# Twenty-six ranges instead of twenty-seven in a planned graph layer: a fourth of the sums per quadrant, fused counting matmuls, and one store set later in the plan

## The chip, the cores and the metric

The kernel runs on one core of one Trainium2 chip. Its time is the device time of that core in microseconds (us), given as the median of many executions; a profile holds one execution, whose span runs from its first to its last instruction. The engines are PE (TensorE, matmuls; PEld is its weight load), DVE (VectorE), ACT (ScalarE), POOL (GpSimd) and SP (SyncE, which here only issues transfers). They run side by side, each through its own list of instructions in order, and wait for one another by semaphores.

## The reference, cut to what matters

A graph has 6250 nodes with 128 features each and 100,000 edges, sorted by their destination. Each edge has one of two types.

```python
Xs = X[src]
m_data = Xs @ W_data.T + b_data
m_ctrl = Xs @ W_control.T + b_control
msg = jnp.where((edge_types == 0)[:, None], m_data, m_ctrl)
agg = jax.ops.segment_sum(msg, dst, num_segments=X.shape[0])
out = relu(agg + (X @ W_self.T + b_self))
x = layernorm(x + out)        # over the 128 features, eps 1e-5
```

A node has 16 incoming edges on average. A message depends only on the source node and the type, so there are 2 x 6250 different messages.

## The kernel before, in words

**The message table.** Up to some 60 us into the run the kernel computes all messages: 49 blocks of 128 nodes, two types, so 98 tiles of 128 rows (`NT`). Each message is kept as three bfloat16 parts of 128 columns side by side, 384 columns (`D3`), whose sum has nearly full precision. The table stays in SBUF as `m3` and is also stored to DRAM as `table`, in 13 pieces (L509). The last piece is the single odd block.

**Two ways to sum.** The nodes are cut in two. The first 27 x 160 = 4320 nodes form 27 ranges ("windows" in the code, `NW` of `WN` = 160 nodes). The other 1930 nodes are cut in 16 blocks of 125 nodes (`GN`), the last one of 55.

*A range* is summed from `m3` by selection matmuls. First the edges of a group of ranges (`GROUPS`: one, then two, then six groups of four) are *ranked* (`ranks`): 21 chunks of 128 edges are turned into one-hot rows over the 98 tiles, and chains of matmuls on `tri` and `rest` (L702) with a maximum on DVE between them (L716) give each edge a slot, at most 32 for each tile. Groups 0 and 1 split the 21 chunks in 4 and 2 chains, and matmuls on `every`, a matrix of ones, add the counts of the earlier chains first. All these matmuls go out as quartets: four matmuls, each with 32 columns of weights, one per quarter (quadrant) of the array's columns. A scatter of 21 matmuls for each range (L752) writes the packed slots to PSUM, ACT copies them to `vs` (L765), and SP stores them to DRAM as `packed` (`put`, L772, L774). SP then loads them back for each range, spread over all partitions (`rows`, L904, 784 KB), and DVE turns them into selection matrices (L912); a second set, `hot2`, comes from L920.

Then `sums` goes over the 25 groups of four tiles (g = 0 to 24, the last with two). Stage 1 (L933) picks the rows with a quartet of 384-column matmuls into a PSUM tile `g`; ACT, at times DVE, copies this to `gs` (L436); stage 2 adds it to the accumulator `a` of the range. The first 128 nodes take a quartet of 384 columns (L947). The remaining 32 nodes take three matmuls of 128 columns (L950), one for each of the three parts; they go to three quadrants, in the columns of the bank behind the first 384. At the end of the range these 96 x 128 values are copied to `bs`, and in `close` a float32 matmul on `fold`, three 32 x 32 identities on top of each other, adds the three parts for the 32 nodes (L552). `close` also adds the own term, the residual and the normalization, and stores the result. The 32 leftover nodes of all ranges of a group are closed together, as a block; the range of group 0 is closed with those of group 1, so there are seven blocks.

*A block of 125 nodes* is summed by gathering (`gathered`): for each 128 edges POOL issues an indirect load of 128 table rows (L1027), into one of 14 `t_msg` buffers, and a quartet on PE adds them to the block's sums by a one-hot matrix (L1034). With some room for the spread of the counts a full block takes 17 such gathers and the last one 8, so 263 in all. Besides these, 14 smaller gathers fetch `sr`, the few edges whose slot did not fit (L861).

**Who sets the order.** `Plan` writes the order of all engines out before the program is built. Every piece of work (`add`) has an engine, a duration, a due time, what it reads and writes. The planner simulates the engines and always lets the engine take the ready piece with the earliest due time; the instructions are then issued in the order of the planned starts. So the durations and due times are no time of the chip, but they set the order. The planned duration of a gather is `GC`; gathers get due times `step` apart, and `step` is the larger of `GC` + 0.02 and the time of the ranges shared out over all gathers. Transfers on SP take 0.45 us in the plan (`SPD`). Some SP transfers with a due time over 60 also have a `slack`: they are ready that much later than their inputs, so that they don't stand at the head of SP's queue waiting. The stores of `packed` are among these, with 2.0; that of group 1 has a due time of 25.7 and so no slack.

## Time and profile before

| | us |
|---|---|
| median of 14 runs | 696.29 (693.05 to 698.5) |
| the profiled execution | 693.26 |
| its span | 691.7 |
| PE busy (matmuls) | 530.7, 77% |
| DVE busy | 398.4, 58% |
| ACT busy | 359.3, 52% |
| POOL busy | 287.6, 42% |
| mean granted clock of TensorE | 0.909 |

Busy time is the time in which at least one instruction of the engine ran. Matmuls overlap, so PE's share says how long PE had work, not how much it got done; for that one counts matmuls in a stretch. A wait is put down to the engine whose semaphore came last. In a row such as `a<-gs,hot 128*32 128x384 bf16 x4` the weights are 128 x 32 and the moving operand is 128 x 384, and x4 is the number of instructions merged in the row. The granted clock is 1.00 or 0.50 in a stretch.

### The profile page before, as it was taken

The numbers are of one execution on the slowest core, as the hardware profiler recorded it, in microseconds if no ns is written. First come the engines' busy times: TensorE is split into PE (matmuls) and PEld (weight loads), VectorE is DVE, ScalarE is ACT, GpSimd is POOL, SyncE is SP. The second block draws the span as 40 slices with busy tenths as digits, with TensorE's granted clock in tenths as the row PEclk, the third lists the DMA queues.
The fourth block names the chain that finished last, engine by engine and source line by source line (L and its number), as shares of the span: only waits on it lengthen the run. The fifth ranks groups of instructions, "written<-read, shape, count | busy, mean of one in ns | idle before, by whom it ended". The sixth has DMA issues, their size and how long they took to land.

```text
span 691.7 us, 26926 instructions
## 1 busy us (share of the span) xinstructions
PE 530.7 (77%) x11461; PEld 374.4 (54%) x11461; DVE 398.4 (58%) x1271; ACT 359.3 (52%) x891; POOL 287.6 (42%) x290
## 2 busy tenths in 40 slices
PE   6999458838778587876878876888778798686893
PEld 4666225626566274654556654666446475464672
DVE  6899336827678185767256674676546374532432
ACT  3657215615456273545545564655446364464783
POOL 1100454264453636355363436445543545553510
PEclk9999677977999699999798999999989999798997
DMA  3797622253423333315234142551414412532311
GB/s 105 225 334 240 196 62 67 51 172 108 134 59 116 87 111 104 116 46 157 78 105 118 50 140 72 144 137 48 154 52 116 124 48 66 179 94 63 109 32 26
DMA packets 63117, 76.83 MB, mean 111 GB/s; under 512 B 21000, under 2 KB 52893, under 8 KB 62989
## 3 DMA queue, kind: packets, MB, share of 16 engines
q1 hardware_dynamic: 49147, 47.35, 22.4%
q0 software_dynamic: 13456, 27.42, 14.6%
q8 instruction: 91, 1.49, 0.9%
q10 hardware_dynamic: 386, 0.26, 0.2%
q14 instruction: 37, 0.30, 0.2%
HBM read 60.50 MB, written 13.17 MB: 107 GB/s over the span
## 4 chain that ended last, share of the span: by engine, by line
PE 68%; ACT 10%; issue 9%; another core or an unknown queue 7%; DVE 3%; DMA 1%; ACTq 0%; DVEq 0%
PE g L933 19%; PE a L947 19%; PE ga L1034 8%; ACT gs L436 8%; PE rk L702 8%; PE a L950 4%; PE vt L752 2%; PE g L493 2%; ACT to_d L443 1%; PE a L493 1%; PE a L518 1%; DVE slot L716 1%; PE ga L702 1%; DMA rows<-packed 1%
## 5 line engine op out<-in xcount | busy, mean ns | idle before, releaser
L436 ACT CAST gs<-g 128x384 bf16<-128x384 f32 x639 | 278.9, 481 | 256.3 <-PE g L933 112.0
L1027 POOL DMA_INDIRECT t_msg<-table,t_idx x263 | 269.1, 1023 | 313.8 <-PE ga L1034 161.5
L947 PE MATMUL a<-gs,hot 128*32 128x384 bf16 x2592 | 263.4, 349 | 98.5 <-ACT gs L436 58.2
L933 PE MATMUL g<-m,rows 128*32 128x384 bf16 x2646 | 277.9, 348 | 15.2 <-issue 13.1
L947 PEld LDWEIGHTS <-hot 128*32 128x32 bf16 x2700 | 124.2, 98 | 169.8 <-issue 150.0
L933 PEld LDWEIGHTS <-rows 128*32 128x32 bf16 x2646 | 164.6, 136 | 37.8 <-issue 24.0
L950 PE MATMUL a<-gs,hot 128*32 128x128 bf16 x1944 | 167.0, 228 | 4.4 <-issue 4.3
L716 DVE TENSOR_REDUCE slot<-rk 128x4 f32<-128x392 f32 (+1 forms) x138 | 77.0, 558 | 113.8 <-PE g L933 39.0
L1034 PE MATMUL ga<-t_msg,t_hot 128*32 128x384 bf16 x1036 | 109.9, 341 | 5.5 <-issue 5.5
L950 PEld LDWEIGHTS <-hot 128*32 128x32 bf16 x2025 | 83.8, 100 | 14.4 <-issue 8.4
L920 DVE TENSOR_TENSOR hot<-iota_b,to_d 128x1280 bf16<-128x1280 bf16 (+1 forms) x81 | 67.3, 841 | 0.0
L702 PE MATMUL rk<-hots,tri 128*32 128x392 bf16 (+1 forms) x588 | 62.1, 327 | 1.4 <-issue 1.4
L702 PE MATMUL rk<-hots,rest 128*32 128x392 bf16 (+1 forms) x556 | 57.5, 331 | 6.2 <-DVE slot L716 3.9
L1021 DVE TENSOR_TENSOR t_hot<-iota_b,t_code 128x768 bf16<-128x768 bf16 (+2 forms) x47 | 24.8, 528 | 58.8 <-PE g L933 31.2
L1034 PEld LDWEIGHTS <-t_hot 128*32 128x32 bf16 x1036 | 48.4, 100 | 18.8 <-issue 14.5
L561 DVE TENSOR_REDUCE s<-a 128x128 f32<-128x384 f32 x27 | 15.0, 557 | 55.4 <-ACT bs L436 37.2
L691 DVE TENSOR_TENSOR hots<-iota_b,st 128x784 bf16<-128x784 bf16 (+1 forms) x83 | 39.1, 488 | 13.0 <-PE rk L702 8.0
L702 PEld LDWEIGHTS <-rest 128*32 128x32 bf16 x624 | 25.6, 98 | 20.4 <-issue 17.8
L912 DVE TENSOR_SCALAR rows<-rows,pid 128x1568 bf16<-128x1568 bf16 x54 | 34.0, 635 | 2.8 <-DMA rows<-packed 2.8
L702 PEld LDWEIGHTS <-tri 128*32 128x32 bf16 x672 | 27.8, 98 | 7.3 <-issue 5.0
L861 POOL DMA_INDIRECT sr<-table,at x14 | 14.4, 1030 | 39.9 <-DVE at L849 26.6
L752 PE MATMUL vt<-hots,two 128*64 128x98 bf16 x546 | 18.8, 209 | 3.3 <-issue 2.8
(188 smaller groups left out, 527.7 us busy)
## 6 DMA issues: line engine op xcount, KB each, us to landing
rows<-packed SPq DMA_DIRECT2D x27, 784.0 KB
table<-m SPq DMA_DIRECT2D x12, 768.0 KB
t_msg<-table,t_idx POOLq DMA_INDIRECT x263
rows<-in_xt SPq DMA_DIRECT2D x8, 256.0 KB
xc<-in_xt SPq DMA_DIRECT2D x6, 320.0 KB
gl<-sr SPq DMA_DIRECT2D x27, 48.0 KB
xr<-in_x SPq DMA_DIRECT2D x5, 256.0 KB
out<-xr SPq DMA_DIRECT2D x5, 256.0 KB
```

The source lines that it names most:

```text
L436: [("ACT", act(cols), lambda: A.copy(o(), src())), ("DVE", dve(cols), lambda: V.tensor_copy(o(), src()))], None, None, due, r, w, lat)
L691: lambda k=k, kn=kn, ci=ci, hs4=hs4: V.tensor_tensor(hv(ci)[:, k - ks[ci] : k - ks[ci] + kn].rearrange("p k w (c d) -> p (k w) c d", d=2), ...
L702: T.matmul(acc.t[R * j : R * j + R, c * wide : c * wide + wide], wt.t[:, R * j : R * j + R], one(k).rearrange("p w c -> p (w c)"), start=s ...
L716: vec(due, len(m) * wide, lambda r=r, m=m: V.tensor_reduce(slot.t[:, r:KT:L, :], acc.t[:, : len(m) * wide].rearrange("p (k w c) -> p k w c ...
L752: T.matmul(vv()[q : q + 64, i // 2, :], two.t[:, (k - k0) * nw + i].rearrange("p f r -> p (f r)"), one(k)[:, i, :], start=k == 0 and i < 2 ...
L912: add("DVE", dve(half * NT, 0.335), lambda sp=sp, rs=rs: V.tensor_scalar(sp.t[:, rs], sp.t[:, rs], pid1.t, None, op0=ALU.is_equal), due - ...
L920: lambda i=i, hot2=hot2, s4=s4, c0=c0, c1=c1: V.tensor_tensor(hot2.t[:, c0:c1].rearrange("p g (c d) -> p g c d", d=2), iota1_b.t.rearrange ...
L933: T.matmul(gp.t[R * t : R * t + R, :D3], sp.t[:, :, 4 * g + t], m3.t[:, 4 * g + t, :], start=True, stop=True)
L947: T.matmul(a.t[R * j : R * j + R, :D3], hot2.t[:, g, R * j : R * j + R], gs.t, start=g == 0, stop=False, skip_group_check=True)
L950: T.matmul(a.t[R * c : R * c + R, D3:], hot2.t[:, g, P:], gs.t[:, c * D : (c + 1) * D], start=False, stop=last, skip_group_check=True)
L1027: add("POOL", GC, lambda m=m, kk=kk: G.indirect_dma_start(out=m.t, out_offset=None, in_=table[:, :], in_offset=bass.IndirectOffsetOnAxis(a ...
L1034: T.matmul(ga.t[R * i : R * i + R, :D3], hot.t[:, k % KB, R * i : R * i + R], m.t, start=k == 0, stop=False, skip_group_check=True)
```

## The change

Seven edits in one:

1. **26 ranges.** `GROUPS` ends in five groups of four and one of three. 26 x 160 = 4160 nodes remain with the ranges; the other 2090 make 17 blocks, sixteen with 17 gathers and one of 90 nodes with 13, so 285 gathers.
2. **Fourths instead of thirds.** The 384 columns of `gs` for the last 32 nodes of a range are cut in four pieces of 96 (`Q`), one for each quadrant, instead of three of 128. The accumulator's tail is 128 x 96.
3. **The fold follows.** `fold` and its two DVE instructions go. In `close`, float32 matmuls on 32-column slices of the identity add the pieces: cut at every multiple of 96 and of 128, there are six segments (96, 32, 64, 64, 32, 96 columns) for each range, where there was one of 128.
4. **Fused counts.** In `ranks` the matmuls on `every` for the chains behind a chunk are one matmul with a repeated operand instead of one for each chain. For group 0 that is 18 quartets of up to 294 columns instead of 36 of 98. Group 1, with two chains, has as many as before.
5. **The planner's gather duration** is 1.26 instead of 1.3, so `step` goes from 1.32 to 1.28.
6. **The planner's durations** for the changed matmuls: stage 2 0.206 instead of 0.22, the block's fold 1.0 instead of 0.6.
7. **The store of group 1's packed slots** gets a slack of 3.0 in the plan.

```diff
-GROUPS = [1, 2] + [4] * 6
+GROUPS = [1, 2] + [4] * 5 + [3]
...
+    Q = D3 // 4
...
-    GC = 1.3
+    GC = 1.26
...
-    fold = C([3 * R, R], F32, "fold")
-    vec(30, R, lambda: V.tensor_add(fold.t, ident.t[: 3 * R, 0:R], ident.t[: 3 * R, R : 2 * R]),
-        [ident], [fold])
-    vec(30, R, lambda: V.tensor_add(fold.t, fold.t, ident.t[: 3 * R, 2 * R : 3 * R]),
-        [ident, fold], [fold])
...
-                for j, (_, bs) in enumerate(block):
-                    T.matmul(o(j, R), fold.t, bs.t, start=True, stop=False, skip_group_check=True)
+                first_ = True
+                for at in sorted({*range(0, D3, Q), *range(0, D3, D)}):
+                    q, f0 = at // Q, at % D
+                    n = min(Q - at % Q, D - f0)
+                    for j, (_, bs) in enumerate(block):
+                        T.matmul(f.t[R * j : R * j + R, f0 : f0 + n],
+                                 ident.t[:, R * q : R * q + R],
+                                 bs.t[:, at % Q : at % Q + n], start=first_, stop=False,
+                                 skip_group_check=True)
+                    first_ = False
...
-            add("PE", 0.6, mms, due, [xb, w_sb, one3, brows, fold] + [b for _, b in block], [f])
+            add("PE", 1.0, mms, due, [xb, w_sb, one3, brows, ident] + [b for _, b in block], [f])
...
-        def add_to(c, wt, k, start, stop):
+        def add_to(c, wt, k, start, stop, n=1):
             for j in range(4):
-                T.matmul(acc.t[R * j : R * j + R, c * wide : c * wide + wide],
-                         wt.t[:, R * j : R * j + R], one(k).rearrange("p w c -> p (w c)"),
-                         start=start, stop=stop, skip_group_check=True)
+                T.matmul(acc.t[R * j : R * j + R, c * wide : (c + n) * wide].rearrange(
+                    "p (n c) -> p n c", n=n), wt.t[:, R * j : R * j + R],
+                    one(k).rearrange("p w c -> p (w c)")[:, None, :].to_broadcast([P, n, wide]),
+                    start=start, stop=stop, skip_group_check=True)
...
-            add("PE", (nc_ - 1 - k // L) * wide / 2400, lambda k=k: [
-                add_to(c, every, k, k == 0 and c == 1, False) for c in range(k // L + 1, nc_)], when + 1.5,
-                [hkey(k), every], [acc])
+            more = nc_ - 1 - k // L
+            add("PE", max(more * wide / 2400, 0.08), lambda k=k, more=more: add_to(
+                nc_ - more, every, k, k == 0, False, more), when + 1.5, [hkey(k), every], [acc])
...
-        add("SP", SPD, put, d2 + 1, [vs], [(packed_b, gi)], lat=2.0)
+        op = add("SP", SPD, put, d2 + 1, [vs], [(packed_b, gi)], lat=2.0)
+        if gi == 1:
+            op.slack = 3.0
...
-                    for c in range(3):
-                        T.matmul(a.t[R * c : R * c + R, D3:], hot2.t[:, g, P:],
-                                 gs.t[:, c * D : (c + 1) * D], start=False, stop=last,
+                    for c in range(4):
+                        T.matmul(a.t[R * c : R * c + R, D3 : D3 + Q], hot2.t[:, g, P:],
+                                 gs.t[:, c * Q : c * Q + Q], start=False, stop=last,
                                  skip_group_check=True)
-                add("PE", 0.22, stage2, d + 0.9, [gs, (hot2, (g >= 9) + (g >= 17))], [a])
+                add("PE", 0.206, stage2, d + 0.9, [gs, (hot2, (g >= 9) + (g >= 17))], [a])
...
-            bs = B(work, [3 * R, D], F32, "bs", 5)
-            evict(lambda bs=bs: bs.t, lambda a=a: a.t[: 3 * R, D3:], D, due + TW + 0.8, [a], [bs])
+            bs = B(work, [P, Q], F32, "bs", 5)
+            evict(lambda bs=bs: bs.t, lambda a=a: a.t[:, D3 : D3 + Q], Q, due + TW + 0.8, [a], [bs])
```

## The prediction

> **What bounds the kernel now.** I read the chain that ended last first, then the costliest groups, then how many matmuls PE got through in stretches of different granted clock, and last two short timelines. The chain and the groups, from the page:
>
> ```profile
> PE 68%; ACT 10%; issue 9%; another core or an unknown queue 7%; DVE 3%; DMA 1%; ACTq 0%; DVEq 0%
> ...
> L436 ACT CAST gs<-g 128x384 bf16<-128x384 f32 x639 | 278.9, 481 | 256.3 <-PE g L933 112.0
> L1027 POOL DMA_INDIRECT t_msg<-table,t_idx x263 | 269.1, 1023 | 313.8 <-PE ga L1034 161.5
> L947 PE MATMUL a<-gs,hot 128*32 128x384 bf16 x2592 | 263.4, 349 | 98.5 <-ACT gs L436 58.2
> L933 PE MATMUL g<-m,rows 128*32 128x384 bf16 x2646 | 277.9, 348 | 15.2 <-issue 13.1
> ```
>
> PE holds 68% of the chain. ACT's copies and POOL's gathers are idle nearly as long as they are busy, and what ends their idle time is PE. So from the end of the table (some 57 us) to 680 us PE's stream of instructions sets the time. How fast PE goes is in the table by stretch (columns: PE busy with its matmuls, PEld, DVE, ACT, POOL, the clock, DMA share, GB/s):
>
> ```profile
> 57.00:680.00 623.00, 479.75 (x10762) 341.72 (x10759) 347.18 (x1051) 327.31 (x827) 283.51 (x277) 0.91 0.36 102
> ...
> 70.00:74.30 4.30, 1.19 (x29) 0.66 (x23) 2.46 (x4) 0.96 (x2) 3.38 (x4) 1.00 1.05 347
> 74.30:88.00 13.70, 7.52 (x97) 4.72 (x100) 4.53 (x10) 3.18 (x8) 4.55 (x5) 0.50 0.45 118
> 98.20:111.90 13.70, 7.28 (x85) 4.22 (x87) 3.67 (x9) 4.61 (x10) 7.14 (x8) 0.50 0.23 59
> ...
> 660.00:680.00 20.00, 19.62 (x520) 16.04 (x511) 6.14 (x25) 17.21 (x44) 0.27 (x1) 1.00 0.10 28
> ```
>
> At the end, with little to wait for, PE does 26 matmuls in a us; over the whole stretch 17.3. The ratio, 1.5, is what waits add to PE's own pace. Part of it are stretches at half clock, in which only 6 to 7 matmuls in a us get done; the first one follows a lull of PE at 70 to 74 us.
>
> The pace itself, from PE's timeline near the end and in the first ranking:
>
> ```profile
> 676.48 0.35 PE L947 MATMUL a<-gs,hot 128*32 128x384 bf16 x4
> 676.64 0.24 PE L950 MATMUL a<-gs,hot 128*32 128x128 bf16 x3
> 676.66 0.38 PE L933 MATMUL g<-m,rows 128*32 128x384 bf16 x4
> 676.86 0.35 PE L947 MATMUL a<-gs,hot 128*32 128x384 bf16 x4
> ```
>
> ```profile
> 11.28 1.79 PE L702 MATMUL ga<-xr,every 128*32 128x98 bf16 x80
> ```
>
> One g takes 0.38 us from L947 to L947. L947 to L950 is 0.16, a quartet of 384 columns; stage 1 is as wide, so the three matmuls of 128 columns take what is left, 0.06. The 80 matmuls on `every` are 20 quartets of only 98 columns; without the last one's own 0.28 us they start within 1.51, 0.079 a quartet. By their columns that would be 0.041 (0.16 x 98/384): short quartets in a row don't go below 0.08.
>
> **The change part by part**, in PE's own time first.
>
> *The range that goes:* 25 g at 0.38, 9.5; its own term, a float32 quartet of 128 columns (two passes; in the groups of the last 25 us a pass of L518 runs 274 ns and the bfloat16 L521 219, 0.055 more, so 0.11 each) and one of bfloat16, 0.28; its 21 scatter and 6 list matmuls, at 24 in 0.56 us (the chain's rows for them), 0.6. The last group keeps its 41 ranking quartets, but at 294 columns instead of 392, 0.04 less each, 1.7. Sum -12.1. ACT loses 25 copies (12 us busy) and DVE the masks and maxima of a range (about 5 us); both have idle time, so I count nothing for them. If ACT were the bound, the 0.41 us that back-to-back copies take at the end would be the price of a g, 25 x 0.41 = 10.3, much the same.
>
> *The gathers that come:* 22 quartets of 384 columns at 0.16, 3.5, and one more own term 0.3: +3.8. POOL issues 22 more at 1.25 us (0.95 and 0.30 of issue), 27.5 us, in the 313.8 it is idle; 14 buffers let it run ahead. That cover is gone only where the plan puts more than 14 gathers behind the last range.
>
> *Fourths instead of thirds:* all four quadrants stream 96 columns, 0.06 x 96/128 = 0.045, so -0.015 for each of 26 x 25 g: -9.8. But it is a fourth pair of weight load and matmul. Bound on the other side: the quartet on `every`, 0.079, which gives +0.019 x 650 = +12.4. I take -9.8, because here a short quartet stands between two of 0.16, in which the weight loads find room, as the three of 0.06 did; the 0.079 is from short quartets alone. The Trainium skill, "TensorE: Matmul & The Clock Gate", section "Wait — 56ns, not 53.3ns?", speaks against this edit: starts of matmuls don't come closer than about 25 ns however few columns they have. By it twelve pairs need 0.30 in a g, which still fits in 0.365, but a fourth that had to be issued alone would cost 0.10 and the edit +26 us.
>
> *The fold:* a block's float32 quartet of 128 columns takes 0.22 now. After, 384 columns in six segments: 0.66 by columns, or, where twelve quartets can't go below 0.079, 0.97. Times seven blocks +3.1 to +5.3; I take +4.2. The two DVE instructions of `fold` (0.36 us, at 9.5 us) ran beside PE: nothing. `bs` is copied with 96 columns instead of 128 (263 ns now): nothing.
>
> *Fused counts:* 36 quartets x 0.079 = 2.8 against six each of 294, 196 and 98 columns, 6 x (0.12 + 0.08 + 0.08) = 1.7: -1.1, in the first 13 us. PE waits there for DVE (6.4 us before the first), so between -1.1 and 0; I take -0.6.
>
> *GC, step and the planner's durations* issue nothing. They put about 3% more gathers beside each range; a new order may shift any wait. Worth 0 to me, with the rival below as its price.
>
> *The store:* SP's timeline (rows L772, L534, L1011, L509, L541, L904):
>
> ```profile
> 62.34 0.33 SPq L772 DMA_DIRECT2D packed<-vs  x1
> 62.77 0.38 SPq L534 DMA_DIRECT2D xr<-in_x  x1
> 63.20 0.42 SPq L1011 DMA_DIRECT2D t_xc<-in_xt  x1
> 63.72 0.38 SPq L509 DMA_DIRECT2D table<-m  x1
> 64.19 0.42 SPq L534 DMA_DIRECT2D xr<-in_x  x1
> 64.66 2.20 SPq L541 DMA_DIRECT2D xr<-in_x  x1
> 66.97 0.83 SPq L904 DMA_DIRECT2D rows<-packed  x2
> ```
>
> With 3 us more in the plan, at 0.45 a transfer, up to six go ahead: the two `xr`, `t_xc`, the table's last piece, one or two of L541. The store would be issued between 63.7 (behind the table's piece) and 67.3, 1.4 to 5.0 later, and `rows` of ranges 1 and 2, at 66.97, as much later less what it stood behind L541 (at most 1.4): +0 to +4. Behind `rows` on SP wait the rest of the `xr` loads and the next `win`; behind its mask on DVE (L912 at 71.39, after 2.81 us of waiting) the ranking of group 2 (L716), for which PE stood 2.25 us until 72.54. So this lies on the path, and nothing that waits for the store gets it earlier, so there is no gain in it: I take +3. In return the table's last piece, 0.43 (one issue) earlier at most, lets the gathers begin earlier; PE uses the first one only at 86 us: nothing. The same page, section "HAM oscillation — how this bites in real kernels", says that an idle gap of PE over about 3.4 us halves its clock. Here the half clock from 74.3 came behind a 2.25 us gap and a thin stretch; by the page a gap of 5 us would bring what the trace has already.
>
> **Sum.** PE's own time: -12.1 + 3.8 - 9.8 + 4.2 - 0.6 = -14.5. In the span that is worth between 1.0 and 1.5 times as much (the ratio above), -14.5 to -21.8; I take -18. With the store's +3: -15. The profiled execution took 693.3, its span 691.7 and 1.6 around it; 678 for such a one. It is 3.0 under the median of the 14 runs, so the forecast is 696.3 - 15 = 681.
>
> **The rivals.**
>
> *The fourth quarter costs a short quartet's pace* (slower). In stage 2, for every g: 0.079 instead of 0.06. Then the PE sum is -14.5 + 9.8 + 12.4 = +7.7, times 1 to 1.5, plus 3: +11 to +15, so 709. It decides from 0.075 a quartet on, where the sum without the store is +5 and no other term makes up for it. For it: the row on `every`. Against it: two 0.16 quartets around.
>
> *More half-clock stretches* (slower). A new order, and a longer lull before range 1, can add them. A stretch of 13.7 us does 97 matmuls, worth 97/17.3 = 5.6 us, so each costs 8; two turn -15 into +1, 697; three make 705. For it: the lull at 70 us grows. Against it: 26 ranges have fewer joints than 27.
>
> *The gathers become the end.* If the plan leaves 25 gathers behind the last range, 11 of them are beyond the 14 buffers: 11 x 1.25 = 14 us at POOL's pace, which eats the gain: 695. Against it: POOL waits for PE 161.5 us.
>
> *The gain hides in other waits.* PE's share shrinks, but ACT's and DVE's rounds set the pace in most stretches, and only the pure removal at half its price shows, -6: 690.
>
> **How the numbers follow.** Forecast 0.52 (its own range 671 to 690), fourth quarter 0.11, half clock 0.15, gathers at the end 0.09, hidden 0.13. A time that differs from before by under 0.2% (1.4 us) can't be told from no change here. Faster: the forecast, the hidden case, and a third of the gathers' case, 0.68. Within 0.2%: another third of it and a fifth of the half-clock case, 0.06. Slower: the rest, 0.26. From 667 (the upper end of the PE sum with the store free and one half-clock stretch fewer: -21.8 - 8) to 704 leaves about 0.1 on each side.
>
> **What would show it.** L950 has four matmuls of 96 columns in a g, and the distance from L947 to L947 near the end is 0.365; at 0.40 the first rival is right. The store stands behind L509 on SP and the first L912 starts at 73 to 75 instead of 71.39. POOL's last gather ends within some 10 us of the last L933. The clock's mean stays near 0.91. Wrong would be the prediction if the half-clock stretches add up to much more or less than now, since they are the largest part of the time that no instruction of the change touches.

## The result and the profile after

The changed kernel takes 722.26 us (median of 10 executions, 719.65 to 724.06) where the kernel before took 696.02 beside it: a ratio of 1.0378, 95% interval 1.0357 to 1.0398. That is 26 us slower, where 15 us faster was forecast, and above the whole range of 667 to 704. The profiled execution has a span of 717.7 us, with a mean granted clock of 0.907 (0.909 before).

The runs below fell on five chips of two kinds. On the first kind, that of the result and of most runs (four of the five), the kernel before takes 695 to 697 us; on the second kind, which is a single chip, it takes 482.5. Every run is therefore compared with runs of the kernel before on the same chip, by their ratio.

The chain that ended last and the costliest groups of the page, after the change (L940, L954, L957, L1034, L1041 and L432 are what L933, L947, L950, L1027, L1034 and L436 were before):

```profile
PE 69%; issue 11%; ACT 9%; another core or an unknown queue 6%; DVE 2%; DMA 1%; SPq 1%; ACTq 0%; DVEq 0%
...
L1034 POOL DMA_INDIRECT t_msg<-table,t_idx x285 | 289.5, 1016 | 331.9 <-PE ga L1041 177.5
L432 ACT CAST gs<-g 128x384 bf16<-128x384 f32 x614 | 268.5, 483 | 274.9 <-PE g L940 117.5
L954 PE MATMUL a<-gs,hot 128*32 128x384 bf16 x2496 | 235.6, 345 | 71.2 <-ACT gs L432 47.5
L940 PE MATMUL g<-m,rows 128*32 128x384 bf16 x2548 | 251.3, 354 | 25.2 <-issue 24.1
```

PE leads the chain as before. L940 lost 27 us of busy time (277.9 to 251.3), yet the span grew, and the share of "issue", time in which an engine waited for nothing that the profile shows, went from 9% to 11%. POOL is still idle for more time than it is busy. So neither the shares nor the groups say where 26 us come from. The ends of the two executions do. Before, the last L933 started at 677.9, no gather was left, and the span ended 13.8 us later:

```profile
659.33 0.94 POOL L1027 DMA_INDIRECT t_msg<-table,t_idx  x1 [0.73 <-PE g L933]
...
677.90 0.34 PE L933 MATMUL g<-m,rows 128*32 128x384 bf16 x2
```

After, the last L940 starts at 686.6, the matmuls of 24 gathers are still to come, ten of the gathers haven't been issued, and the span ends 31.1 us later. PE's timeline and POOL's from the last L940 on, after the change:

```profile
686.55 0.36 PE L940 MATMUL g<-m,rows 128*32 128x384 bf16 x2
...
687.86 0.95 POOL L1034 DMA_INDIRECT t_msg<-table,t_idx  x1 [0.60 <-PE ga L1041]
...
689.11 0.95 POOL L1034 DMA_INDIRECT t_msg<-table,t_idx  x1 [0.30 <-issue]
...
690.36 0.95 POOL L1034 DMA_INDIRECT t_msg<-table,t_idx  x1 [0.30 <-remote]
690.73 0.42 PE L552 MATMUL vt<-bs,ident 128*32 128x32 f32 x5 [0.47 <-issue]
...
692.22 0.24 PE L552 MATMUL vt<-bs,ident 128*32 128x96 f32 x1 [1.06 <-issue]
...
692.94 0.27 PE L552 MATMUL vt<-bs,ident 128*32 128x96 f32 x1 [0.48 <-issue]
693.65 1.09 PE L514 MATMUL vt<-w_sb,xb 128*32 128x128 f32 x4 [0.44 <-issue]
...
701.12 0.95 POOL L1034 DMA_INDIRECT t_msg<-table,t_idx  x1 [0.30 <-issue]
...
703.77 3.70 PE L1041 MATMUL ga<-t_msg,t_hot 128*32 128x384 bf16 x39 [4.57 <-DVE s L565]
```

Two things are to be seen. POOL issues gathers 1.25 us apart with no range left beside them. And the fold of the last block, which needs no gather, crawls: PE starts one or a few matmuls, stands 0.4 to 1.1 us on "issue", starts the next.

The tail, from the last stage 1 to the end, is 17.3 us longer, of the 26. The other 8.7 lie ahead of it: 26 ranges end 8.7 us later than 27 did. The prediction's gain is absent there as well. PE's matmuls by stretch, after (columns as in the table before):

```profile
57.00:680.00 623.00, 482.99 (x11211) 314.48 (x11204) 339.57 (x1042) 310.34 (x786) 289.46 (x285) 0.91 0.36 102
...
680.00:718.00 38.00, 16.07 (x277) 9.21 (x276) 9.66 (x43) 8.24 (x21) 13.52 (x15) 0.72 0.22 58
```

PE gets 18.0 matmuls done in a us up to 680, against 17.3 before, but there are more of them for each g, twelve instead of eleven.

### The profile page after: what moved, and what is told of

Same layout as the page of the kernel before. It is cut to its first block, busy times and chain, and to the rows that moved or that the text cites. A ratio compares the mean times of both kernels' runs of the same rounds, so it can differ in the third digit from the quotient of the medians.

```text
span 717.7 us, 28174 instructions
## 1 busy us (share of the span) xinstructions
PE 548.3 (76%) x12088; PEld 354.7 (49%) x12088; DVE 395.2 (55%) x1276; ACT 348.0 (48%) x864; POOL 307.1 (43%) x312
## 4 chain that ended last, share of the span: by engine, by line
PE 69%; issue 11%; ACT 9%; another core or an unknown queue 6%; DVE 2%; DMA 1%; SPq 1%; ACTq 0%; DVEq 0%
PE g L940 20%; PE a L954 18%; PE ga L1041 9%; ACT gs L432 7%; PE rk L706 7%; PE a L957 4%; PE vt L757 2%; PE g L489 2%; ACT to_d L439 1%; PE vt L552 1%; PE a L489 1%; PE a L514 1%; DMA win<-in_edges 1%; PE ga L706 1%
## 5 line engine op out<-in xcount | busy, mean ns | idle before, releaser
L1034 POOL DMA_INDIRECT t_msg<-table,t_idx x285 | 289.5, 1016 | 331.9 <-PE ga L1041 177.5
L432 ACT CAST gs<-g 128x384 bf16<-128x384 f32 x614 | 268.5, 483 | 274.9 <-PE g L940 117.5
L954 PE MATMUL a<-gs,hot 128*32 128x384 bf16 x2496 | 235.6, 345 | 71.2 <-ACT gs L432 47.5
L940 PE MATMUL g<-m,rows 128*32 128x384 bf16 x2548 | 251.3, 354 | 25.2 <-issue 24.1
L954 PEld LDWEIGHTS <-hot 128*32 128x32 bf16 x2600 | 114.3, 100 | 150.2 <-issue 130.0
L957 PE MATMUL a<-gs,hot 128*32 128x96 bf16 x2496 | 159.4, 213 | 10.2 <-issue 10.0
L721 DVE TENSOR_REDUCE slot<-rk 128x4 f32<-128x392 f32 (+2 forms) x138 | 75.0, 544 | 147.9 <-PE rk L706 66.0
L940 PEld LDWEIGHTS <-rows 128*32 128x32 bf16 x2548 | 108.6, 138 | 62.8 <-issue 41.0
L1041 PE MATMUL ga<-t_msg,t_hot 128*32 128x384 bf16 x1127 | 103.9, 347 | 13.7 <-issue 8.5
L957 PEld LDWEIGHTS <-hot 128*32 128x32 bf16 x2600 | 86.1, 99 | 31.7 <-issue 20.8
L706 PE MATMUL rk<-hots,tri 128*32 128x392 bf16 (+2 forms) x588 | 54.4, 326 | 3.5 <-issue 3.5
L1041 PEld LDWEIGHTS <-t_hot 128*32 128x32 bf16 x1127 | 40.2, 104 | 32.0 <-issue 26.1
L706 PE MATMUL rk<-hots,rest 128*32 128x392 bf16 (+2 forms) x556 | 50.7, 325 | 5.7 <-issue 4.4
L695 DVE TENSOR_TENSOR hots<-iota_b,st 128x784 bf16<-128x784 bf16 (+3 forms) x83 | 37.8, 474 | 13.7 <-remote 9.9
L565 DVE TENSOR_REDUCE s<-a 128x128 f32<-128x384 f32 x26 | 14.5, 557 | 50.0 <-ACT bs L432 18.9
L706 PEld LDWEIGHTS <-rest 128*32 128x32 bf16 x624 | 21.1, 100 | 18.1 <-issue 15.2
```

The costliest lines, as they stand in the source:

```text
L432: [("ACT", act(cols), lambda: A.copy(o(), src())), ("DVE", dve(cols), lambda: V.tensor_copy(o(), src()))], None, None, due, r, w, lat)
L695: lambda k=k, kn=kn, ci=ci, hs4=hs4: V.tensor_tensor(hv(ci)[:, k - ks[ci] : k - ks[ci] + kn].rearrange("p k w (c d) -> p (k w) c d", d=2), ...
L706: T.matmul(acc.t[R * j : R * j + R, c * wide : (c + n) * wide].rearrange("p (n c) -> p n c", n=n), wt.t[:, R * j : R * j + R], one(k).rear ...
L721: vec(due, len(m) * wide, lambda r=r, m=m: V.tensor_reduce(slot.t[:, r:KT:L, :], acc.t[:, : len(m) * wide].rearrange("p (k w c) -> p k w c ...
L940: T.matmul(gp.t[R * t : R * t + R, :D3], sp.t[:, :, 4 * g + t], m3.t[:, 4 * g + t, :], start=True, stop=True)
L954: T.matmul(a.t[R * j : R * j + R, :D3], hot2.t[:, g, R * j : R * j + R], gs.t, start=g == 0, stop=False, skip_group_check=True)
```

## The experiments

Five accounts were set against each other. A, the tail: gathers left behind the last range cost what they take. B, crowding: gathers back to back slow PE down while they run. C: one of the other edits (fourths, fold, store) costs it. D: every gather stops PE for a while, crowded or not. E: PE is slow for another reason, and the gathers only happen at the same time.

| run | chip | us | ratio, 95% interval | from last stage 1 to the end |
|---|---|---|---|---|
| after, 27 ranges | first | 710.91 | 1.021 (1.0168 to 1.0252) | 13.6 |
| before, 26 ranges | first | 717.47 | 1.031 (1.026 to 1.036) | 37.8 |
| after, store not later | first | 724.26 | 1.0414 (1.0365 to 1.0463) | 31.4 |
| before, fourths and fold | first | 709.95 | 1.017 (1.0105 to 1.0235) | 14.0 |
| before, pause 0.54 us | second | 573.98 | 1.1921 (1.182 to 1.2023) | 14.1 |
| after, pause 0.54 us | second | 598.34 | 1.242 (1.2316 to 1.2524) | 50.2 |
| after, GC 1.0 | second | 536.3 | 1.1149 (1.1039 to 1.1259) | 15.1 |
| after, unaltered | second | 507.47 | 1.052 (1.0478 to 1.0562) | 32.9 |
| before, half the gathers | second | 475.67 | 0.986 (0.9826 to 0.9893) | 14.0 |
| after, GC 1.13 | first | 709.81 | 1.0212 (1.0165 to 1.0259) | 15.1 |
| before, 26 ranges, GC 1.13 | first | 696.47 | 1.0024 (0.999 to 1.0057) | 14.8 |
| before, fourths and fold | first | 707.87 | 1.0155 (1.0085 to 1.0225) | 14.3 |
| before, half the gathers | first | 559.13 | 0.8013 (0.797 to 0.8057) | 13.9 |
| before, pause 0.54 us | first | 636.84 | 0.9152 (0.91 to 0.9204) | 14.0 |
| before, 26 ranges, GC 1.13 | first | 697.11 | 1.0023 (0.999 to 1.0056) | 14.8 |
| before, fourths and fold | first | 710.94 | 1.019 (1.0136 to 1.0244) | 14.2 |
| before, pause 0.27 us | first | 682.8 | 0.9808 (0.9765 to 0.9851) | 13.9 |
| after, pause 0.27 us | first | 713.34 | 1.0261 (1.0227 to 1.0295) | 30.5 |

The last column is from each run's trace. It is 13.6 to 15.1 us wherever no gather is left behind the last range, and 30 to 50 where some are.

**The change with 27 ranges again.**

```diff
-GROUPS = [1, 2] + [4] * 5 + [3]
+GROUPS = [1, 2] + [4] * 6
```

> The changed kernel with 27 ranges again (GROUPS back to 1, 2 and six of 4); all other edits stay. Theory A (the tail): what makes the changed kernel late is that gathers are left behind the last range. In the changed kernel the last L940 ends at 686.6 with 24 of 285 gather quartets to come, and the span ends 31.1 us later; before, the last L933 ends at 677.9 and the span 13.8 later. With 27 ranges there are 263 gathers, and the planner's order puts none of them behind the last range, as before: so the tail is some 14 us again, and the time falls by at least the 17 us of the tail, to 695 to 707. Theory B (the bursts): what costs is that PE does some 6 matmuls in a us, instead of some 20, whenever POOL issues four or more indirect gathers back to back (11 such runs of gathers with 82.8 us of PE's time before, 13 with 107.0 after). By it the time goes by the length of these runs: 695 to 710 if they shrink to some 83 us, about 720 if they stay at 107. Theory C (the edits of the fourths, the fold or the store cost it): they are all still in, so 717 to 730.

710.91, a little above what A (to 707) and B (to 710) gave. The tail is gone, as A has it, and the ranges and what is edited in them still cost 2.1%. So the range that went accounts for a part of the loss only.

**The kernel before with 26 ranges, alone.**

```diff
-GROUPS = [1, 2] + [4] * 6
+GROUPS = [1, 2] + [4] * 5 + [3]
```

> The kernel before with GROUPS alone changed to 26 ranges (the last group has 3); GC stays at 1.3, thirds, fold and store stay. The planner's order puts 22 gathers behind the last range here (16 in the changed kernel, none before). Theory A (the tail): this one edit is enough: 712 to 730, with a span that ends 28 to 38 us behind the last L933. Theory B (the bursts): slower by what the runs of back-to-back gathers grow; with 107 us of them some 715 to 720, with 83 us about 690. Theory C (fourths, fold or store): none of them is in, so the range that went shows as a gain: 680 to 690.

717.47: this one edit, with nothing else, loses 21 us. At the last L933 the matmuls of 30 gathers are to come, and the end is 37.8 us away, at the upper edge of what A expected.

**The changed kernel without the store's slack.**

```diff
-        if gi == 1:
-            op.slack = 3.0
```

> The changed kernel without the later place of the packed store of the second group; all else stays. My prediction gave the store +3 (0 to 4). In the changed kernel the store left SP at 67.29 (62.34 before), and the rows of ranges 1 and 2 at 68.87 (66.97). Theory A and theory B: the store has little part in the loss: 718 to 724, as with the store. Theory C in its form for the store: 700 to 712. The store would be seen ahead of L509's last piece again and the rows at some 67.

724.26, not faster than the changed kernel: the two intervals overlap. The store's place is worth nothing that these runs can tell.

**Fourths and fold alone**, 27 ranges. The planner's durations of edit 6 stay in, so the plan lays other instructions in another order too.

```diff
+    Q = D3 // 4
...
-                    for c in range(3):
-                        T.matmul(a.t[R * c : R * c + R, D3:], hot2.t[:, g, P:],
-                                 gs.t[:, c * D : (c + 1) * D], start=False, stop=last,
+                    for c in range(4):
+                        T.matmul(a.t[R * c : R * c + R, D3 : D3 + Q], hot2.t[:, g, P:],
+                                 gs.t[:, c * Q : c * Q + Q], start=False, stop=last,
...
-            bs = B(work, [3 * R, D], F32, "bs", 5)
+            bs = B(work, [P, Q], F32, "bs", 5)
```

> The kernel before with the fourths and the fold of segments alone: 27 ranges, GC 1.3, counts and store as before. My prediction gave the fourths -9.8 and the fold +4.2, -5.6 in PE's own time and up to -8.4 in the span. The profile of the changed kernel speaks against it: from one g to the next the distance is 0.380 there as before, though L957 itself is 0.015 shorter; the following quartet takes 0.18 instead of 0.163. So I expect the fourths at 0 and the fold at +3 to +6: 696 to 703. With the gain as predicted it would be 688 to 692; if the fourth quarter were the whole loss, 715 to 725. What the bursts do under another plan is the unknown of it, some 8 us either way.

> The kernel before with the fourths and the fold of segments alone, as in the run that took 709.95 (696.13 for the kernel before beside it). There PE's starts, counted from one to the next where that is at most 0.3 us, gave L954 38.7 us for 2684 starts where L950 had 34.9 for 2010, and L552 6.7 for 1.8: +3.8 and +4.9 of PE's own, nothing of the predicted -9.8; the gaps behind these two lines were 39.9 us against 13.7. On a chip like the second, where gathers bring no gaps, PE's own is left: 1.01 to 1.02 of the kernel before, 488 to 493. If the loss on the first chip was only an unlucky order, 480 to 487. On a chip like the first 704 to 712 again.

> The kernel before with the fourths and the fold of segments alone, once more, for a chip of the second kind: 1.00 to 1.01 of the kernel before (482 to 487) if what it cost on the first kind (707.87 and 709.95 with 695.63 and 696.13 beside them) was mostly gaps, 488 to 496 if it was PE's own. On a chip of the first kind 704 to 712 again.

709.95, 707.87 and 710.94 on three chips of the first kind: ratios with a mean of 1.0172, 12.0 us. The predicted -5.6 is refuted, and so is, as a time, my later +3 to +6 for the two. What the two cost on the second kind was not seen. PE's timeline of the changed kernel shows that the fourths bring no gain where nothing disturbs them:

```profile
669.24 0.35 PE L954 MATMUL a<-gl,hot 128*32 128x384 bf16 x4
669.40 0.23 PE L957 MATMUL a<-gl,hot 128*32 128x96 bf16 x4
669.45 0.36 PE L940 MATMUL g<-m,rows 128*32 128x384 bf16 x4
669.62 0.35 PE L954 MATMUL a<-gs,hot 128*32 128x384 bf16 x4
669.78 0.23 PE L957 MATMUL a<-gs,hot 128*32 128x96 bf16 x4
```

From L954 to L954 it is 0.38, as from L947 to L947 before. There L933 started 0.02 behind the three matmuls and the next L947 0.20 behind L933; here it is 0.05 and 0.17. Over all stretches with this pattern the median distance is 0.38 in both. What the narrower quartet saves is lost in the quartets around it: PE's time from start to start, where that is at most 0.3 us, adds up for the three lines of stages 1 and 2 to 262.6 us before and to 264.5, 260.1 and 262.9 in the three runs, so the fourths are worth nothing in PE's own time. For the fold the same count goes from 1.8 us to 6.7, 5.9 and 6.6, +4.6 in the mean. The remaining 7 of the 12 us are gaps of over 0.3 us. In these runs 7.3 to 7.8 us of gaps stand behind the fold's matmuls, and 0.4 in the kernel before; but with 26 ranges and the old fold it is 4.5 and 6.1, so where a gap falls is no property of the line. The three runs are of one program and so have one order, in which DVE's instructions follow each other otherwise than before. Whether the 7 us belong to the fold, to the fourths or to that order no run separates: it stays open.

**A pause behind every gather.**

```diff
+    pause = C([P, 448], I32, "pause")
...
+                    G.iota(pause.t, pattern=[[1, 448]], base=0, channel_multiplier=0)
```

> The kernel before, with one more instruction on POOL behind each gather of messages: an iota into a scratch tile of 448 int32 columns that nothing reads. Gathers can then no longer follow each other at 1.25 us; the duration of this iota is in no row so far, and it uses more of POOL's 314 us of idle time. Theory B in its strong form (gathers back to back are what slows PE): the 82.8 us in which PE did some 6 matmuls a us go at a faster pace; 640 to 685. Theory B in its weak form (PE and the run of gathers both come late because POOL stood behind an sr gather that waited for DVE; the gathers only catch up): PE then waits for each gather longer than before, and the time goes up by what the pauses make the refilling of the 14 buffers longer, 11 runs of some 5 gathers: 700 to 740.

> The changed kernel with the same pause behind each gather. Strong form of theory B: 655 to 700, and the tail shorter too, since the fold matmuls there ran at 0.4 to 1.06 us each with no dependence on a gather. Weak form: 725 to 770, with the tail longer by 24 pauses.

These fell on the second kind, where the kernel before takes 482.51. There PE waits 52.9 us for gathered rows, and POOL, with its pauses, is busy for 438.3 us of a span of 573.4; both kernels lose. The first was repeated, on the first kind:

> The kernel before with an iota of 0.54 us behind each gather, once more, for a chip of the first kind: gathers are 1.8 us apart at the closest, and 263 of them take some 490 us of POOL. Theory D with a fixed gap for each gather, whatever their distance: 690 to 705. Theory B (the harm is in the crowding: 19 to 20 matmuls in a us with one gather in the last 2.5 us, 11 with two): 640 to 685. On a chip of the second kind again 572 to 576, since there POOL becomes the bound.

636.84, 59 us *faster* than the kernel before, just under what B expected, though POOL does the same gathers and 140 us of iota besides. What it changes is seen in a burst. First the kernel before, three stretches in which POOL issues gathers back to back (columns: PE busy with its matmuls, PEld, DVE, ACT, POOL, clock, DMA share, GB/s), then two stretches of the same lengths at about the same points in the kernel with the pause:

```profile
90.00:104.00 14.00, 6.73 (x90) 2.83 (x79) 3.39 (x8) 1.72 (x4) 10.48 (x11) 0.79 0.30 77
143.00:155.00 12.00, 3.40 (x31) 1.15 (x31) 0.00 (x0) 1.16 (x3) 8.99 (x10) 0.62 0.36 107
225.00:236.00 11.00, 4.94 (x39) 1.85 (x40) 1.12 (x3) 0.96 (x2) 8.25 (x9) 0.63 0.39 110
```

```profile
139.00:151.00 12.00, 10.18 (x223) 7.24 (x220) 8.97 (x27) 6.38 (x17) 10.97 (x14) 0.91 0.47 137
222.00:233.00 11.00, 7.93 (x158) 4.51 (x151) 5.10 (x19) 4.02 (x11) 9.83 (x14) 1.00 0.51 174
```

With ten gathers in 12 us PE got 31 matmuls done, DVE none, ACT three. Where gathers and pauses take turns, seven of each, PE got 223 done in as long. Only the pauses were added, and the time fell: so the crowd of gathers is a cause, not a companion, and E falls. Half-clock stretches add up to 29.9 us here and to 127.9 in the kernel before, so most of these came with the crowds of gathers and went with them. The Trainium skill, "TensorE: Matmul & The Clock Gate", section "HAM oscillation — how this bites in real kernels", has idle gaps of over some 3.4 us as what halves the clock; these two sums agree in direction, and no run here varied the length of a gap alone.

**Half of the gathers left out.**

```diff
+                    if kk % 2:
+                        G.memset(m.t, 0.0)
+                        return
```

> The kernel before with every second gather of messages left out: its tile is filled with zeros by POOL instead, so half of the messages are missing from the sums; the plan's order and all other instructions stay. Theory D (a gap of PE for each gather, on a chip like the first): 131 gathers fewer at some 0.8 us, 575 to 610. Theory B in its weak form (PE and the gathers are both late for another reason): 680 to 700. On a chip like the second, where the kernel before takes some 482, theory D expects 470 to 485.

> The kernel before with every second gather of messages left out (zeros from POOL in its place, so half of the messages are missing from the sums), once more, since the first time it fell on a chip of the second kind (475.67 with 482.72 beside it). On a chip of the first kind (the kernel before at some 696): theory D, a gap of PE for each gather, 131 gaps at some 0.8 us fewer, 575 to 610. Theory E (PE and ACT are slow there for a reason that has nothing to do with the gathers, which only catch up at the same time): 685 to 697. On a chip of the second kind again 473 to 478.

On the second kind 475.67, 7 us less than the kernel before; on the first kind 559.13, 137 us less, 1.04 us for each of the 131 gathers left out. D expected some 105 (131 at 0.8) and is too small; that crowds cost more, which it left out, would explain it. E expected 685 at the least.

Counted in the traces: PE's matmuls in a us, by how many gathers began in the 2.5 us ahead (from 85 us on, without the last 25 us; in the last row only some 12 us have none).

| trace | none | one | two |
|---|---|---|---|
| before, first kind | 24.2 | 19.1 | 10.8 |
| after, first kind | 26.1 | 20.0 | 11.6 |
| before, half the gathers, first kind | 25.9 | 21.6 | 12.9 |
| before, pause 0.54, first kind | 26.1 | 18.1 | 18.7 |
| after, second kind | 24.7 | 27.0 | 27.8 |

**The changed kernel, unaltered, on the second kind.**

> The changed kernel unaltered, once more. The chip of the pause runs took 482.5 us for the kernel before, and PE's pace there did not fall behind gathers (25 matmuls in a us with two gathers in the last 2.5 us; in the first profiles 11 with two, 19 to 20 with one, 24 to 26 with none). Theory D: on the first chips every gather stops PE for some 0.8 us, so PE's time is its work plus its gaps (starts more than 0.3 us apart, from 60 us on: 272 with 235.8 us before, 356 with 270.2 us in the changed kernel; the rest 385.6 and 377.3). If this chip is like the first, 718 to 726 again, 1.033 to 1.042 of the kernel before. If it is like the second, the gaps that gathers bring fall away and the 8 us of PE's work that the change saves are left: 0.97 to 0.99 of the kernel before by theory D; by theory A (the tail) 1.01 to 1.04, since 24 gathers at 1.25 us behind the last range are POOL's own pace on any chip.

507.47, a ratio of 1.052: it loses 24.8 us also where gathers don't stop PE. D expected 0.97 to 0.99 here and fails; A expected up to 1.04 and has the sign. The tail is 32.9 us, 18.9 more than the 14.0 that the run with half the gathers has on this kind. The other 6 lie ahead of it: the last L940 starts at 473.0, and in the kernel before, of which there is no trace on this kind, the last stage 1 would start at some 467 (an estimate: 482.7 less the 1.6 around the span and a tail of 14.0). So the gain of the range that went is missing on this kind as well. PE's and POOL's timeline in the tail:

```profile
489.39 0.95 POOL L1034 DMA_INDIRECT t_msg<-table,t_idx  x1 [0.30 <-issue]
489.53 0.51 PE L1041 MATMUL ga<-t_msg,t_hot 128*32 128x384 bf16 x3 [0.46 <-DMA t_msg<-table,t_idx]
...
490.64 0.95 POOL L1034 DMA_INDIRECT t_msg<-table,t_idx  x1 [0.30 <-issue]
490.81 0.51 PE L1041 MATMUL ga<-t_msg,t_hot 128*32 128x384 bf16 x3 [0.77 <-DMA t_msg<-table,t_idx]
...
491.89 0.95 POOL L1034 DMA_INDIRECT t_msg<-table,t_idx  x1 [0.30 <-issue]
492.11 0.51 PE L1041 MATMUL ga<-t_msg,t_hot 128*32 128x384 bf16 x3 [0.80 <-DMA t_msg<-table,t_idx]
```

PE waits for each gather: the end runs at POOL's 1.25 us. This is the plainest view of A.

**Gathers laid earlier by the plan.** `GC` issues nothing; with 1.26 the last 16 gathers of the changed kernel are planned behind the last range, with 1.0 and 1.13 none.

```diff
-    GC = 1.26
+    GC = 1.0
```

> The changed kernel with GC at 1.0 in place of 1.26, which issues nothing and changes the plan's order alone: gathers stand earlier on POOL, none behind the last range. Theory A (the tail): the tail is 14 us again, 700 to 706. If the gathers that no longer stand in the tail make the ranges slower by as much (26 ranges end 21 us later in the changed kernel although they are as many as 26 of 27 before), the time stays at 715 to 725.

On the second kind 536.3: the tail is 15.1 as A wants, but the last L940 starts at 519.8 instead of 473.0. The plan asks there for gathers faster than POOL's 1.25, and PE waits for them among the ranges: 31.1 us up to the last range, where the unaltered changed kernel waits 2.6 (the rest of its 12.9 is the tail). That is most of the 46.8; the remainder was not traced. PE's longest sum of waits, with 1.0 and in the unaltered changed kernel on the same kind (us, times, longest):

```profile
PE ga L1041 <- DMA t_msg<-table,t_idx: 32.4, 23, 3.1
```

```profile
PE ga L1041 <- DMA t_msg<-table,t_idx: 12.9, 14, 2.9
```

The middle value, on the first kind, with the change and with nothing of it but the 26 ranges:

> The changed kernel with GC at 1.13 in place of 1.26; nothing else. The plan then lays gathers 1.15 apart instead of 1.28: 285 of them end ahead of the last range, as the 263 did before the change, and are less crowded at the beginning than with 1.0. Theory A (the tail): on the second chip the changed kernel had its last L940 at 473.0 and its end at 505.8, 32.8 later, with 24 gather quartets to come; if these stand earlier, the tail is the 14 us of before, so 485 to 492 (1.005 to 1.02 of the kernel before), and on a chip like the first 700 to 707. If the earlier gathers push the ranges back by as much, as with 1.0 (536, its last L940 at 519.8 on that chip), 505 to 540, and 718 to 730 on the first.

> The kernel before with two edits: 26 ranges, and GC at 1.13, so that no gather is planned behind the last range. Thirds, fold, counts and store stay as before. If the range that goes is worth what I had said for it (-12.1 and +3.8 in PE's own time, -8.3), and only the tail ate it, then 470 to 480 on a chip like the second (0.975 to 0.995 of the kernel before), and 676 to 692 on one like the first by theory A; by theory D, on a chip like the first the 22 gathers more cost 22 gaps of 0.8, 17.6, so 690 to 710. If it is slower by over 2% on the second chip, a crowd of gathers costs PE there too.

> The kernel before with 26 ranges and GC at 1.13, once more, for a chip of the second kind. On one of the first kind it gave 696.47 with 695.63 beside it: the range that went was worth nothing, and the tail was gone. On a chip of the second kind the 22 gathers more bring no gaps, so the -8.3 of PE's own time shows: 470 to 480. If the gathers cost there in another way (late transfers, as with GC at 1.0), 485 to 500.

With GC 1.13 the changed kernel goes from 1.0378 to 1.0212, 11.6 us, not quite the 700 to 707 of A; its tail shrinks by 16.0 while its last range ends 6.5 later. The kernel before with 26 ranges goes from 1.031 to 1.0024 and, on another chip, 1.0023: 20 us, nearly all of the 21 that the edit had lost, and no more. So on the first kind a range less is worth +1.6 us, not measurably different from nothing, once its gathers don't stand in the tail. That is inside D's bounds (690 to 710) and above A's (676 to 692). No run has 27 ranges with GC at 1.13, so what the denser order costs by itself isn't known, and no run has this kernel on the second kind.

**Half the pause**, for both kernels:

```diff
-    pause = C([P, 448], I32, "pause")
+    pause = C([P, 224], I32, "pause")
...
-                    G.iota(pause.t, pattern=[[1, 448]], base=0, channel_multiplier=0)
+                    G.iota(pause.t, pattern=[[1, 224]], base=0, channel_multiplier=0)
```

> The kernel before with half the pause: an iota of 224 columns, some 0.27 us, behind each gather, so that gathers are at least 1.5 us apart. On a chip of the first kind the pause of 0.54 us gave 636.84 with 695.9 beside it. Theory B (crowding): a part of that, 645 to 680. If even 1.5 us apart is as crowded as 1.25: 690 to 700. On a chip of the second kind POOL needs 263 x 1.53, 402 us, of some 390 in which gathers go there: 485 to 515.

> The changed kernel with the same 0.27 us behind each gather. Theory A (the tail) says that the change loses with the pause too: 24 gathers behind the last range at 1.53 us instead of 1.25, so 22 to 30 more than the kernel before with this pause; theory B alone (the change is slower only since it has more crowded gathers): at most 10 more. On a chip of the first kind 670 to 710, on one of the second 515 to 545.

682.8 and 713.34. The shorter pause keeps 1.9% of the 8.5% that the longer one gave, a little less than expected. The changed kernel loses 30.5 us to the kernel before also with spread gathers, just above A's 22 to 30 and far from B alone (at most 10). But only 16.6 of them are the tail, 30.5 us against 13.9; the other 13.9 lie ahead of it, about what the fourths and the fold cost by themselves (12.0). So the tail is confirmed, and A alone is not the whole.

The kernel before with the pause of 0.54 us beats both kernels on the first kind by 8.5%, and loses 19% on the second. No version here beats both on both kinds.

## Why the prediction was wrong

By the runs of the first kind the loss of 26.2 us is made up of the fourths with their fold, 12.0 (mean of three runs), the tail, 11.6 (GC 1.13 against 1.26), and the range, 1.6 (two runs). Together 25.2, if they simply add, which no run tests. The 11.6 is less than the 17.3 by which the tail grew, since gathers taken out of it cost the ranges ahead something. All three answer to terms or rivals of the prediction.

*The gathers that come: hidden, "in the 313.8 it is idle".* This step failed most plainly, and its own condition says how: the cover was to be gone "only where the plan puts more than 14 gathers behind the last range". It put 24 there, by their matmuls, and POOL's last gather, which was to end within some 10 us of the last stage 1, ended 15.5 behind it. A sum of idle time over the whole span covers nothing at its end. The diff had the sign of it: a `step` of 1.28 for 285 gathers is 365 planned us, and the 26 ranges have 338; before it was 1.32 x 263 = 347 in 351 (a range has 13 in the plan). All of these numbers were at hand, and I did not multiply them. The rival "the gathers become the end" describes this case well (25 gathers, 14 us, where the tail grew by 17.3); its chance of 0.09 and its 695, which took the other gains for given, were wrong.

*Fourths: -9.8.* Nothing of it came. The test I named, L947 to L947 at 0.365, reads 0.38; 0.40, the first rival's reading, isn't there either. My argument that a quartet's time is its columns was right for the quartet and wrong for the g: before, L933 already started 0.02 behind the three matmuls, and 0.05 behind the four: what the idle quadrant left free was used already. The trace of before showed these starts, in the lines that I quoted. *The Trainium skill's floor of 25 ns a start* ("TensorE: Matmul & The Clock Gate", section "Wait — 56ns, not 53.3ns?") doesn't explain it: in the second kind's run a start of L957 is followed by the next start after 14.2 ns in the mean, less than that floor, and the g takes 0.38, not 0.30 or 0.48.

*The fold: +4.2.* Right in PE's own starts: +4.6 on the first kind; on the second the starts take 5.5 us in the changed kernel and 1.5 in the run with half the gathers, +4.0. (Its upper bound should have been +5.1: twelve quartets at 0.079 are 0.95, not 0.97.) With the fourths at nothing, 4.6 of the +12.0 of the two edits are the fold's starts, where -5.6 was forecast for both; the rest are gaps that no term of the sum held, and whose cause stays open.

*The range that goes: -12.1 and +3.8, times 1.0 to 1.5.* Measured +1.6 in place of -8.3 to -12.5. The step that failed is the price of a gather, taken as its quartet of 0.16: on the first kind leaving out 131 of them gave 1.04 us each. At 0.8 to 1.04 us (an estimate from the gaps and from that run) 22 more gathers cost 18 to 23 us, more than the range that they replace could bring. That they ate it is argued, not shown: no run adds gathers and nothing else, and on the second kind, where a gather left out gave 0.05 us, the gain is missing too. The trace of before held a sign of it: 19 matmuls in a us with one gather in the 2.5 us ahead and 11 with two, against 24 with none. I had read "the ratio, 1.5, is what waits add" as a mean over waits of no owner, and took the stretches at half clock as given; most of them went when the gathers were spread.

*The store: +3.* It left SP behind the table's last piece, as foreseen. SP's timeline, rows L505 (table), L537, L777 (store), L911 (`rows`):

```profile
64.37 0.38 SPq L505 DMA_DIRECT2D table<-m  x1
64.84 0.92 SPq L530 DMA_DIRECT2D xr<-in_x  x1
65.81 1.38 SPq L537 DMA_DIRECT2D xr<-in_x  x3
67.29 0.38 SPq L777 DMA_DIRECT2D packed<-vs  x1
...
68.87 0.81 SPq L911 DMA_DIRECT2D rows<-packed  x2
```

5.0 us later than before, at the end of my bound, and `rows` 1.9 later. But the first mask came at 86.3, not at 73 to 75, and at 80.2 in the run without the slack, whose store left at 62.9: most of that delay is another's, and without the slack the whole took no less time (724.26). The store is late as foreseen; its price is not seen.

*Fused counts: -0.6.* The first `every` matmuls start behind DVE at 6.43, before at 6.41, and the matmuls on `tri` that follow the last of them start at 12.94, before at 12.90: nothing was won.

*More half-clock stretches.* They add up to 135.9 us against 127.9. But 23.3 and 11.8 of these begin behind the last stage 1; ahead of it there are 112.6 against 116.1, so this rival has no part in what the ranges lost.

## What to carry to other kernels

Idle time of a queue hides its new work only where the work's place in the order lets it: add up the planned pace of what is added against the time that is left, and look at what stands behind the last piece of the engine that ends. Before a wait is called a fact of the engine, count that engine's pace by what the others did in the microseconds ahead; one table of it, from the trace of before, would have pointed at the gathers, and a run that leaves half of them out prices them. A cheaper instruction is worth what the distance from one round to the next becomes, and the starts within a round show whether there was a hole to fill.

## What the runs showed of the hardware that was not expected

On the first kind of chip indirect gathers stop PE. It does 24 to 26 matmuls in a us without one, 11 with two in the 2.5 us ahead, 31 matmuls in 12 us in a crowd of ten; PE stands there in the middle of a quartet, on "issue", and ACT and DVE do nearly nothing either; whether they are stopped too or only wait for PE was not separated. On the second kind the same program runs without it (27 or 28 matmuls in a us with one or two gathers): the two lines below are the changed kernel from 200 to 300 us, first kind and second kind.

```profile
200.00:300.00 100.00, 77.62 (x1873) 50.38 (x1862) 62.00 (x194) 51.33 (x129) 48.48 (x46) 0.97 0.36 103
```

```profile
200.00:300.00 100.00, 94.57 (x2810) 74.19 (x2810) 89.35 (x276) 74.37 (x193) 75.43 (x73) 1.00 0.52 145
```

Half as many matmuls again, and more than half as many gathers again. A gather's 0.95 us on POOL and ACT's copy of 0.48 us are the same on both, so it is not the speed of these two engines that differs. Spreading the gathers by 0.54 us won 59 us on the first kind. What in a gather does it (its descriptors, its transfers, its signals) and what makes the two kinds of chips differ, of which the second is a single chip, was not found: no run separates them, and it stays open.
